# A transformer block on one core: another order of the preparation, and where three batches' MLP rows are normalised and turned

## The chip, the cores and the metric

The kernel runs on one core of a Trainium2 chip. The metric is the device time of one execution in microseconds (us), lower is better. An execution has five engines that run side by side, each through its own list of instructions: TensorE (PE), VectorE (DVE), ScalarE (ACT), GpSimd (POOL) and SyncE (SP), which here only sends transfers (DMAs).

## The reference, cut to what matters

There are 16 batches of 256 tokens with 256 features, 16 heads of 16, an MLP of 1024, and a context of 256 tokens for each batch. All in float32.

```python
c_proj = silu(c) @ W_mod + b_mod
shift_a, scale_a, gate_a, shift_m, scale_m, gate_m = split(c_proj, 6)
modulate = lambda t, shift, sc: t * (1 + sc[:, None]) + shift[:, None]

qkv = modulate(ln(x), shift_a, scale_a) @ W_qkv + b_qkv          # self attention
x = x + gate_a[:, None] * (attention(qkv) @ W_proj + b_proj)

q_c, kv_c = ln(x) @ W_qc + b_qc, ln(context) @ W_kvc + b_kvc      # cross attention
x = x + attention(q_c, kv_c) @ W_cproj + b_cproj

h = gelu(modulate(ln(x), shift_m, scale_m) @ W_mlp1 + b_mlp1)     # MLP
x = x + gate_m[:, None] * (h @ W_mlp2 + b_mlp2)
```

## The kernel before

**Products.** A float32 operand is cut in a high part (a type that TensorE multiplies in one pass) and a low part (the rest). A product is then three: high by high, high by low, low by high. `xTh` and `xTl` are the two parts of a batch's normalised rows, turned so that features lie on the partitions; `Wq`, `Wk`, `Wv` and the others are pairs (high, low). An operand that is turned by TensorE goes through PSUM with a tile named `psT_...`.

**Three stages.** (1) A *preparation* turns the condition, makes the modulation's columns, splits the first weights and makes Q, K and V of the first units. (2) 32 *units* follow, 16 of self attention ("s") and 16 of cross attention ("c"), each with eight beats; beat k of unit n makes scores for unit n+1 (`s`), exponentials' inputs for unit n (`st`), and pieces of the products of units around them. Q and K stand in three big buffers `big[0..2]`, in rows that transfers fill from tiles `h_q`, `l_q`, `h_k`, `l_k` (high and low parts); the fourth kind of row, and all that is not written, is zero, so that each buffer is filled with zeros first. (3) The *MLP* of 16 batches follows in 64 chunks of 256 hidden features: a chunk has the first product (`ph`, twelve matmuls), the GELU (twice on ACT, `hf` and `hh`, and the difference `hl` on POOL) and the second product (twelve matmuls into `s` or `st`). Chunks 0 to 6 of batches 0 and 1 are begun in the last units.

**The order is written out by hand.** Every engine runs its instructions in the order of the program. Strings of words hold that order, and each word issues one step on whatever engines it needs:

- `PRE` is the preparation. `load` sends the first loads from SP; `ld2` loads the third batch; `lg`, `lc`, `lp` load weights that are used later; `z0kp`, `z0qp` and so on fill a half of a big buffer with zeros on POOL (suffix p) or ACT (suffix a; a copy of a zero tile); `bN` runs N warm-up matmuls of zeros on TensorE; `silu` and `turn` make `sT`, the turned silu of the condition (times 1/2); `L0a` and `L0b` are the layer norm's statistics and its `rs` (a power on POOL), `L0d` the normalised rows on DVE; `scale`, `sc1` and `shift` make the modulation's columns `cpT`; `T0t`, `T0h`, `T0l` turn the rows and cut them; `hik`, `lok` split W_k; `K0a`, `K0m` are the two halves of K's product, `K0h`, `K0l` its high and low rows, `K0x`, `K0yp`, `K0w` the three transfers (p: sent by POOL). `bk`, `bq`, `bv` make the biases that the shift adds.
- `SL` places further steps after given beats; `(-1, k)` are the beats before the first unit.
- `BE` is the seam from the attention to the MLP: `Gj`, `Fj`, `Sj` are GELU, first and second product of chunk j; `xb`, `bb`, `sb`, `pb`, `ab` load batch b's rows, add a bias row to them, take the statistics, the power, and the normalised rows; `Tb` turns them by TensorE, `rb` and `gb` are residual and gates; `aT aL C CF` belong to the last attention.

After `BE` a loop runs over the chunks from 12 on. In it a batch's rows are turned in one of two ways, by `TURN`: below it by TensorE (`mlp_T`, four turns, after rows that ACT normalised), from it on without TensorE (`mlp_turn`: DVE transposes blocks of 32 x 32, and four transfers move the blocks; `mlp_scaled` and `mlp_rows` then make both parts).

Loads and stores go through SP's one queue. The tiles of `big`, `wself` and `wcross` are used again by the MLP: `wcross` holds its rows (`ROWS`), `big[2]` the second weights.

Of the kernel before, what the change touches and what calls it, by code (L numbers as in the profile page):

```python
# [16 lines left out]
P = 128  # L17
# [4 lines left out]
def pixart_block(  # L22
# [31 lines left out]

    E_ = {'CUT': 8, 'LN': {'s': 'pool', 'c': 'pool', 'q': 'pool'}, 'ON': (1, 1, 1), 'L0': -16, 'L1': 1, 'S0': -7, 'A0': 0, 'T0': 1, 'S1': 5, 'A1': 7, 'L2': 9, 'T1': 9, 'S2': 32, 'AP': 99, 'DV': (0, 1), 'HP': (1, 0), 'BZ': {}, 'AV': {1: [(1, 2), (1, 3)], 9: [(0, 0), (0, 1)]}, 'AHEAD': (0, 0, 0, 0, 0, 2), 'TW': {(21, 6): 'cb', (23, 5): 'u0', (23, 7): 'u1', (25, 2): 'u2', (27, 3): 'u3', (27, 7): 'h2a', (28, 0): 'l2 h0p u5', (28, 2): 'h1p', (28, 4): 'h3p', (28, 7): 'u4 u6', (29, 0): 'l3d', (29, 1): 'l0', (29, 2): 'l1', (29, 7): 'h5p', (30, 1): 'u7 h6d h7p', (30, 3): 'h4p', (31, 1): 'l4 l6d', (31, 2): 'l5d x2', (31, 4): 'l7', (31, 7): 'b2'}, 'BE': 'G0 av P g0 A1 G1 G2 N1 F7 g1 S0 PF s2 p2 G3 a2 aT aL G4 x3 b3 S1 S2 T2 C r0 G5 S3 G6 S4 s3 CF x4 F8 g2 G7 S5 F9 p3 S6 G8 a3 r1 G9 F10 G10 T3 g3 b4 x5 x6 S7 s4 F11 S8 S9 F12 G11 p4 a4 F13 r2 S10 G12', 'XP': 1, 'IL': 1, 'MF': 0, 'SH': 4, 'RAMP': 1, 'HA': 1, 'MP': 16, 'W': (7, 1, 0, 0), 'PRE': 'load L0a z0kp z0qp L0b silu b15 hik turn L0d brow bp z1qa lok T0t lg scale b1 lc sc1 bro2 T0h T0l shift b3 ld2 one0 hiq loq L1a hiv K0a L1b bk K0m L1d bq K0h K0l Q0a L2a T1t T1h lp K0yp K0x z1kp Q0m T1l bv K1a Q0h K0w Q0x Q0yp Q0l lov K1b Q1a Q0w L2b Q1b K1l V0a K1y Q1l z2ka ld3', 'SL': {(-1, 0): 'V0b wm one1 L2c', (-1, 1): 'V1a T2t T2h', (-1, 2): 'K1wp T2p', (-1, 3): 'K1xp L3a Q1yp V1b ga', (-1, 4): 'M0 z2qa Q1xp Q1wp pb L3b vone gs', (-1, 5): 'mods0 ld4', (-1, 6): 'K2a K2m L3p', (-1, 7): 'L3c cb lx gm', (0, 0): 'sp3 mods1', (0, 1): 'sp0', (0, 3): 'sp1', (0, 4): 'sc2', (0, 6): 'one2', (1, 1): 'sp2', (1, 2): 'sp4'}}

# [41 lines left out]
    BQ, BK, BQC, BKC = 32, 34, 36, 38  # L98
    c_sb, th = [work.tile([B, 2, H], F32, tag=t, name=n, bufs=3)[:, 0] for t, n in (("qkh", "c_sb"), ("qkl", "th"))]
    SP.dma_start(c_sb, cond)  # L100
# [84 lines left out]
    def f_silu():  # L185
        ACT.activation(dummy, mhalf, AF.Tanh)
        ACT.activation(th, c_sb, AF.Tanh, scale=0.5)
        DVE.scalar_tensor_tensor(th, th, 1.0, c_sb, ALU.add, ALU.mult)

    def f_turn():  # L190
        pst = st[:, 1, 480:]
        for k in range(KC):
            PE.transpose(pst[:, k * B:(k + 1) * B], th[:, k * P:(k + 1) * P], ident[:B, :B])
        ACT.mul(sT.rearrange("p k b -> p (k b)"), pst[:, :KC * B], 0.5)

# [102 lines left out]
    wm = []  # L298
# [224 lines left out]
    def to_stack(W, src, bias, dst, which, name):  # L523
# [8 lines left out]
        def first():  # L532
            o.ps = ps_gen(f"ps_{name}", LONG)
            mm3(o.ps[:, 0:N], W, 0, src.xT)

        def third():
# [362 lines left out]

    TURN = 6  # L900

# [85 lines left out]
    def mlp_second(b, c):  # L987
# [15 lines left out]
        if done and b < B - 1:  # L1003
            for t in range(NT):
# [8 lines left out]

    steps = {"x": mlp_load, "b": mlp_bias, "s": mlp_stats, "p": lambda b: M[b].ln.pow(), "a": mlp_apply,
             "r": mlp_residual, "g": mlp_gates, "T": mlp_T, "F": lambda j: mlp_first(j // NCH, j % NCH),
             "G": lambda j: mlp_gelu(j // NCH, j % NCH), "S": lambda j: mlp_second(j // NCH, j % NCH)}
# [46 lines left out]
    for n, v in (("0", u0), ("1", u1), ("2", u2)):  # L1063
        word["T" + n + "t"], word["T" + n + "h"], word["T" + n + "l"] = v.T[0].parts
        word["T" + n + "p"] = v.T[0].low_pool
        for c in "KQ":
            o = getattr(v, c)
            word[c + n + "l"] = o.parts[2]
            word[c + n + "m"], word[c + n + "h"] = o.third, o.high
# [11 lines left out]
    for n in range(3):  # L1081
        for h, c in enumerate("qk"):
            for e, q in (("", DVE), ("p", POOL)):
                word[f"z{n}{c}{e}"] = lambda n=n, h=h, q=q: q.memset(big[n][:, h].bitcast(F32), 0.0)
            word[f"z{n}{c}a"] = lambda n=n, h=h: ACT.copy(
                big[n][:, h].rearrange("p k (a c) -> p (k a) c", c=P),
                wz.unsqueeze(1).to_broadcast([P, 16, P]))
# [12 lines left out]
    word["vone"] = lambda: [POOL.memset(v[:, :, :, HD:], 1.0) for v in vts]  # L1100
    for n, f in (("load", f_load), ("silu", f_silu), ("turn", f_turn), ("brow", f_brow), ("bp", f_bp), ("bro2", f_bro2),
                 ("scale", f_scale), ("sc1", f_sc1), ("shift", f_shift),
# [187 lines left out]
    for i, (b, c) in list(enumerate(chunks))[12:]:  # L1290
# [90 lines left out]
```

## Time and profile before

| what | value |
|---|---|
| runs | 727.61, 727.65, 729.59 us; median 727.65 |
| the profiled execution | 728.29 us; span from its first to its last instruction 726.5 us; mean granted TensorE clock 0.997 |
| PE busy | 718.9 us (99%), 10086 matmuls |
| PE weight loads busy | 633.3 us (87%) |
| DVE busy | 567.8 us (78%) |
| ACT busy | 579.3 us (80%) |
| POOL busy | 526.8 us (73%) |
| DMA | 90.56 MB, mean 125 GB/s |

How to read it: the profile gives the busy time of each engine, and the chain of work that ended last, followed back from the last instruction. Nearly all source lines are those of one helper (line 51), so instructions are told apart by their tiles, written output<-inputs. "PE" is TensorE's matmuls, "PEld" its weight loads, "SPq" and "POOLq" the sequencers that issue transfers. A number in front of a tile's name in a timeline is the start in us from the span's start, then the time that the group took. In square brackets stands the idle time of the engine ahead of the group and what ended it. The granted clock is the share of TensorE's full clock that the chip allowed.

### The profile page before, as it was taken

Reading aid. Unit: us, or ns where it says so; the run is one execution under the profiler, and the core shown is the slowest. Engines: PE = TensorE matmul, PEld = TensorE weight load, DVE = VectorE, ACT = ScalarE, POOL = GpSimd, SP = SyncE. Lnnn points to the kernel's source line nnn. Section 1 sums busy time; section 2 is a strip of 40 time slices with the busy share of each in tenths; the row PEclk is TensorE's granted clock in tenths of the full one; section 3 lists DMA queues with packets and bytes.
Section 4 is the critical chain, followed back from the end, with each engine's and each line's share of the span. In section 5 each row is a group of like instructions: output and inputs, shape, how many; then the busy total and the mean of one; then the engine's idle time right before and its main releaser. Section 6 shows DMA issues by size and latency. Waiting matters only on the chain.

```text
span 726.5 us, 24914 instructions
## 1 busy us (share of the span) xinstructions
PE 718.9 (99%) x10086; PEld 633.3 (87%) x10086; DVE 567.8 (78%) x1208; ACT 579.3 (80%) x1006; POOL 526.8 (73%) x561
## 2 busy tenths in 40 slices
PE   9999999999999999999999999999999999999997
PEld 8788888888888888888888888888878999999997
DVE  4888898989888888888889888888845675676552
ACT  5578898888888888888888888898887677777773
POOL 6766687969687786969687898979746756656643
PEclk9999999999999999999999999999999999999999
DMA  6645333332424343342433444244311414334421
GB/s 208 209 150 176 119 120 143 138 120 105 162 107 161 124 152 124 120 147 112 169 119 137 152 149 161 106 145 142 128 52 54 117 46 117 96 87 111 102 64 39
DMA packets 67110, 90.56 MB, mean 125 GB/s; under 512 B 6194, under 2 KB 38740, under 8 KB 66996
## 3 DMA queue, kind: packets, MB, share of 16 engines
q1 hardware_dynamic: 66164, 86.88, 35.8%
q8 instruction: 80, 1.31, 0.7%
q0 software_dynamic: 560, 1.84, 0.7%
q14 instruction: 34, 0.28, 0.1%
q10 hardware_dynamic: 272, 0.26, 0.1%
HBM read 26.97 MB, written 8.46 MB: 49 GB/s over the span
## 4 chain that ended last, share of the span: by engine, by line
PE 93%; POOL 3%; issue 1%; DVE 1%; ACT 1%; DMA 0%; POOLq 0%; ACTq 0%
PE s L51 18%; PE o L51 16%; PE st L51 15%; PE ph L51 10%; PE ps_P_s L51 4%; PE ps_qc L51 4%; PE ps_v_c L51 4%; PE ps_kc L51 4%; PE ps_q L51 4%; PE ps_v_s L51 3%; PE ps_k L51 3%; PE ps_P_c L51 2%; PE psT_q L51 1%; PE psA_s L51 1%; POOL hl L51 1%
## 5 line engine op out<-in xcount | busy, mean ns | idle before, releaser
L51 DVE TENSOR_REDUCE mx<-s 128x2 f32<-128x512 f32 x504 | 324.7, 683 | 64.3 <-PE s L51 59.0
L51 ACT ACTIVATE pt<-st 128x1024 f32<-128x1024 f32 x252 | 258.9, 1028 | 16.9 <-PE st L51 10.5
L51 PE MATMUL s<-big 63*128 63x256 f32 (+1 forms) x1024 | 185.6, 299 | 0.2
L51 PEld LDWEIGHTS s<-big 63*128 63x128 f32 (+1 forms) x1024 | 133.5, 186 | 19.1 <-DVE l_kc L51 6.6
L51 PE MATMUL st<-big 64*128 64x256 f32 (+1 forms) x1024 | 134.4, 299 | 0.5 <-DMA big<-l_q 0.3
L51 POOL TENSOR_TENSOR hl<-hf,hh 128x512 fp32r<-128x512 f32 x64 | 87.4, 1368 | 63.2 <-ACT hh L51 63.1
L51 PE MATMUL o<-pt,v 128*32 128x256 f32 x2048 | 123.8, 382 | 0.0
L51 PEld LDWEIGHTS st<-big 64*128 64x128 f32 (+1 forms) x1024 | 96.3, 187 | 16.0 <-issue 13.0
L51 PEld LDWEIGHTS o<-pt,v 128*32 128x32 f32 x2048 | 60.0, 109 | 41.4
L51 PE MATMUL ph<-wcross,wself 128*128 128x256 f32 x672 | 85.4, 277 | 0.0
L51 PEld LDWEIGHTS ph<-wcross,wself 128*128 128x128 f32 x672 | 80.4, 188 | 0.0
L51 ACT COPY oT<-o 128x512 f32<-128x512 f32 x63 | 37.0, 587 | 32.7 <-PE o L51 32.7
L51 ACT ACTIVATE hf<-ph,bT 128x256 f32<-128x256 f32 x114 | 47.7, 472 | 18.4 <-PE ph L51 18.4
L51 ACT ACTIVATE hh<-ph,bT 128x256 fp32r<-128x256 f32 x114 | 47.9, 473 | 17.9 <-PE s L51 8.7
L51 PE MATMUL ps_kc<-xTh_c,wcross 64*128 64x256 f32 x256 | 46.6, 291 | 0.0
L51 PE MATMUL s<-big,hh 128*128 128x256 f32 x256 | 45.2, 277 | 0.0
L51 PE MATMUL st<-big,hh 128*128 128x256 f32 x256 | 45.2, 277 | 0.0
L51 PE MATMUL ps_v_c<-wcross,xTh_c 64*128 64x256 f32 x256 | 44.3, 292 | 0.0
L51 PE MATMUL ps_k<-xTh_s,wself 64*128 64x256 f32 (+1 forms) x232 | 43.5, 293 | 0.0
L51 PE MATMUL ps_qc<-xTh_q,wcross 64*128 64x256 f32 x256 | 41.2, 280 | 0.0
L51 PE MATMUL ps_q<-xTh_s,wself 64*128 64x256 f32 (+1 forms) x240 | 40.7, 287 | 0.0
L51 POOL TENSOR_SCALAR xn_c<-c,mv_c,rs_c 128x256 f32<-128x256 f32 x32 | 39.0, 1227 | 1.7
(240 smaller groups left out, 2135.7 us busy)
## 6 DMA issues: line engine op xcount, KB each, us to landing
big<-h_kc SPq DMA_DIRECT2D x32, 256.0 KB
big<-h_qc SPq DMA_DIRECT2D x32, 256.0 KB
big<-h_k SPq DMA_DIRECT2D x30, 256.0 KB
big<-h_q SPq DMA_DIRECT2D x29, 256.0 KB
g<-gd SPq DMA_DIRECT2D x16, 256.0 KB
c<-in_ctx_dram SPq DMA_DIRECT2D x16, 256.0 KB
big<-l_kc SPq DMA_DIRECT2D x16, 256.0 KB
big<-l_qc SPq DMA_DIRECT2D x16, 256.0 KB
```

What stands on the lines that cost most here:

```text
L51: i = f(*a, **k)
```

## The change

*In the preparation* the condition is turned by TensorE before the silu, not after it: `silu` now issues the two turns, and Tanh and the halving on ACT work on the turned 128 x 32 columns; a new step `th2` makes the product on DVE. POOL fills one half buffer and a half of another (`z0kp`, `z1kAp`) ahead of the power, where it filled two; ACT fills a half buffer (`z1qa`) right after the silu, and another (`z0qa`) later. The first K is made by new steps `K0i` (the four high-by-high products, both halves) and `K0j` (the other eight), with the shift columns between them; then follow `bk`, `K0h` and so on. The loads `ld2`, `lg`, `lc`, `lp` are all issued ahead of the transfers of K. The statistics of the third batch (`L2a`) move from before to after the first Q. The warm-up matmuls go from `b15`, `b1`, `b3` to `b5`, `b3`, `b1`, `b1`.

*In the seam* the rows of batches 2 and 4 are normalised by ACT (new words `N`, two small steps on POOL that make -mean x rs, and `e`) instead of by DVE (`a2`, `a4`). Batch 4's bias, statistics and power move ahead; batch 5's bias, statistics, power and `N` are added.

*In the loop* `TURN` is 5 instead of 6: batch 5 is turned by DVE and transfers, no longer by TensorE.

```diff
-'BE': 'G0 av P g0 A1 G1 G2 N1 F7 g1 S0 PF s2 p2 G3 a2 aT aL G4 x3 b3 S1 S2 T2 C r0 G5 S3 G6 S4 s3 CF x4 F8 g2 G7 S5 F9 p3 S6 G8 a3 r1 G9 F10 G10 T3 g3 b4 x5 x6 S7 s4 F11 S8 S9 F12 G11 p4 a4 F13 r2 S10 G12'
+'BE': 'G0 av P g0 A1 G1 G2 N1 F7 g1 S0 PF s2 p2 N2 G3 aT aL e2 G4 x3 b3 S1 S2 T2 C r0 G5 S3 G6 S4 s3 CF x4 F8 g2 G7 S5 F9 p3 S6 G8 a3 r1 G9 F10 b4 G10 T3 g3 x5 x6 s4 p4 N4 S7 F11 S8 S9 F12 G11 e4 b5 F13 r2 S10 s5 G12 p5 N5'
-'PRE': 'load L0a z0kp z0qp L0b silu b15 hik turn L0d brow bp z1qa lok T0t lg scale b1 lc sc1 bro2 T0h T0l shift b3 ld2 one0 hiq loq L1a hiv K0a L1b bk K0m L1d bq K0h K0l Q0a L2a T1t T1h lp K0yp K0x z1kp Q0m T1l bv K1a Q0h K0w Q0x Q0yp Q0l lov K1b Q1a Q0w L2b Q1b K1l V0a K1y Q1l z2ka ld3'
+'PRE': 'load z0kp b5 silu L0a th2 z1kAp L0b z1qa b3 brow bp L0d scale sc1 b1 T0t hik lok T0h bro2 b1 K0i T0l shift K0j z1kBp hiq loq ld2 lg one0 lc lp z0qa L1a L1b bk L1d K0h hiv K0l Q0a bq K0yp K0x T1t T1h K0w Q0m T1l Q0h bv K1a Q0x Q0yp Q0l Q0w lov L2a K1b Q1a L2b Q1b K1l V0a K1y Q1l z2ka ld3'
...
     def f_silu():
         ACT.activation(dummy, mhalf, AF.Tanh)
-        ACT.activation(th, c_sb, AF.Tanh, scale=0.5)
-        DVE.scalar_tensor_tensor(th, th, 1.0, c_sb, ALU.add, ALU.mult)
-
-    def f_turn():
         pst = st[:, 1, 480:]
         for k in range(KC):
-            PE.transpose(pst[:, k * B:(k + 1) * B], th[:, k * P:(k + 1) * P], ident[:B, :B])
-        ACT.mul(sT.rearrange("p k b -> p (k b)"), pst[:, :KC * B], 0.5)
+            PE.transpose(pst[:, k * B:(k + 1) * B], c_sb[:, k * P:(k + 1) * P], ident[:B, :B])
+        ACT.activation(th[:, :KC * B], pst[:, :KC * B], AF.Tanh, scale=0.5)
+        ACT.mul(th[:, KC * B:2 * KC * B], pst[:, :KC * B], 0.5)
+
+    def f_th2():
+        DVE.scalar_tensor_tensor(sT.rearrange("p k b -> p (k b)"), th[:, :KC * B], 1.0, th[:, KC * B:2 * KC * B],
+                                 ALU.add, ALU.mult)
...
+        def some(products):
+            for n, (a, k, f) in enumerate(products):
+                PE.matmul(o.ps[:, f * N:(f + 1) * N], W[a // 2][:, k, f * P:(f + 1) * P], src.xT[a % 2][:, k],
+                          start=(a == n == 0), stop=(a == 2 and k == KC - 1), skip_group_check=True)
+
+        def high_high():
+            o.ps = ps_gen(f"ps_{name}", LONG)
+            some([(0, k, f) for k in range(KC) for f in range(2)])
+
+        def rest():
+            some([(a, k, f) for a in (1, 2) for k in range(KC) for f in range(2)])
+
+        o.by_part = high_high, rest
...
-    TURN = 6
+    TURN = 5
...
+             "N": lambda b: M[b].ln.shift(), "e": lambda b: M[b].ln.steps[2]("act"),
...
+            for i, part in enumerate("AB"):
+                word[f"z{n}{c}{part}p"] = lambda n=n, h=h, i=i: POOL.memset(
+                    big[n][:, h, 4 * i:4 * i + 4].bitcast(F32), 0.0)
...
-            if TURN < b + 4 < B:
+            if 6 < b + 4 < B:
                 mlp_load(b + 4)
```

More of the change, by code (lines that the diff above doesn't have):

```diff
@@ L98, in pixart_block @@
     BQ, BK, BQC, BKC = 32, 34, 36, 38
-    c_sb, th = [work.tile([B, 2, H], F32, tag=t, name=n, bufs=3)[:, 0] for t, n in (("qkh", "c_sb"), ("qkl", "th"))]
+    c_sb, th = [work.tile([p, 2, H], F32, tag=t, name=n, bufs=3)[:, 0]
+                for p, t, n in ((B, "qkh", "c_sb"), (P, "qkl", "th"))]
     SP.dma_start(c_sb, cond)
@@ L1068, in pixart_block @@
             word[c + n + "l"] = o.parts[2]
+            word[c + n + "i"], word[c + n + "j"] = o.by_part
             word[c + n + "m"], word[c + n + "h"] = o.third, o.high
@@ L1100, in pixart_block @@
     word["vone"] = lambda: [POOL.memset(v[:, :, :, HD:], 1.0) for v in vts]
-    for n, f in (("load", f_load), ("silu", f_silu), ("turn", f_turn), ("brow", f_brow), ("bp", f_bp), ("bro2", f_bro2),
+    for n, f in (("load", f_load), ("silu", f_silu), ("th2", f_th2), ("brow", f_brow), ("bp", f_bp), ("bro2", f_bro2),
                  ("scale", f_scale), ("sc1", f_sc1), ("shift", f_shift),
```

2 lines of the change are left out of this document (1 added, 1 removed).

## The prediction

> **What bounds the kernel now.** I read the page first, for the busy shares and the chain that ended last.
>
> ```profile
> PE 718.9 (99%) x10086; PEld 633.3 (87%) x10086; DVE 567.8 (78%) x1208; ACT 579.3 (80%) x1006; POOL 526.8 (73%) x561
> PE 93%; POOL 3%; issue 1%; DVE 1%; ACT 1%; DMA 0%; POOLq 0%; ACTq 0%
> ```
>
> TensorE is the bound: it is busy 99% of the span and holds 93% of the chain. A change pays only where TensorE waits, works at a reduced clock, or has work taken away. To find those places I read the busy time by stretches.
>
> ```profile
> 4.89:8.30 3.41, 3.23 (x28) 2.82 (x27) 0.95 (x3) 2.01 (x5) 2.66 (x4) 1.00 1.01 328
> 39.03:42.44 3.41, 3.41 (x39) 3.41 (x38) 1.98 (x3) 2.22 (x4) 2.48 (x4) 0.50 0.63 243
> 582.00:717.00 135.00, 135.00 (x1193) 135.00 (x1192) 82.83 (x172) 101.77 (x242) 78.41 (x73) 1.00 0.33 85
> ```
>
> Columns: stretch, its length, busy us (and instructions) of PE, PEld, DVE, ACT, POOL, then granted clock. The last 135 us have TensorE full to the hundredth, so whatever it is spared there, or before it, shows at the end. The middle row is a stretch of 3.41 us in which the granted clock was 0.50. The first row looks busy but is not product work: much of it is waiting turns and warm-up matmuls. So the two places to look at are the preparation and the seam before the last 135 us. Here is the preparation, by the timeline (start, length, engine, operation, count, then the idle time before it and its releaser).
>
> ```profile
> 1.04 5.44 PE L51 MATMUL s<-wz 128*128 128x128 f32 x30 [1.04 <-DVE wz L51]
> 1.79 3.55 POOL L51 MEMSET big<- 128x2048 f32 x2
> 3.18 0.41 ACT L51 ACTIVATE th<-c_sb 16x256 f32<-16x256 f32 x1 [0.47 <-DMA c_sb<-in_cond_dram]
> 3.81 0.75 DVE L51 BATCH_NORM_STATS2 st_s<-x 128x6 f32<-128x256 f32 x2 [2.56 <-DMA x<-in_x_dram]
> 4.48 0.30 DVE L51 BATCH_NORM_AGGREGATE mv_s<-st_s 128x2 f32<-128x6 f32 x2
> 5.42 0.23 POOL L51 TENSOR_SCALAR rs_s<-mv_s 128x2 f32<-128x2 f32 x1
> 5.73 0.71 POOL L51 TENSOR_TENSOR rs_s<-rs_s,mhalf 128x2 f32<-128x2 f32 x1
> 6.29 0.66 ACT L51 CAST wself<-wf 128x512 fp32r<-128x512 f32 x1 [2.70 <-DMA wf<-in_L_xcond_W_qkv_dram]
> 6.48 0.74 DVE L51 TENSOR_SCALAR xn_s<-x,mv_s,rs_s 128x256 f32<-128x256 f32 x2 [1.38 <-POOL rs_s L51]
> 6.86 0.18 ACT L51 ACTIVATE sT<-st 128x32 f32<-128x32 f32 x1
> 7.34 1.89 ACT L51 CAST big<-wz 128x2048 fp32r<-128x2048 f32 x1
> 9.58 0.84 ACT L51 ACTIVATE xTh_s<-psT_s,sc 128x256 fp32r<-128x256 f32 x2
> 10.45 0.88 DVE L51 SCALAR_TENSOR_TENSOR xTl_s<-psT_s,sc,xTh_s 128x256 fp32r<-128x256 f32 x2 [1.08 <-ACT xTh_s L51]
> 12.76 0.19 DVE L51 TENSOR_TENSOR bqkv<-st,bT 128x32 f32<-128x32 f32 x1 [0.47 <-PE st L51]
> 13.57 0.84 ACT L51 ACTIVATE h_k<-ps_k,bqkv 128x256 fp32r<-128x256 f32 x2 [2.07 <-PE ps_k L51]
> 17.41 0.87 DVE L51 SCALAR_TENSOR_TENSOR l_q<-ps_q,bqkv,h_q 128x256 fp32r<-128x256 f32 x2
> 20.25 2.44 POOL L51 TENSOR_SCALAR xn_s<-x,mv_s,rs_s 128x256 f32<-128x256 f32 x2
> ```
>
> From the chain in order of time, the lengths of TensorE's groups, and the transfer at its end:
>
> ```profile
> 6.96 0.87 PE psT_s L51 x4
> 11.88 0.84 PE st L51 x8
> 14.37 0.81 PE ps_q L51 x6
> 15.18 0.45 PE psT_s L51 x4
> 18.30 2.69 DMA big<-l_q
> 21.13 0.50 PE st L51 x4
> 23.87 0.45 PE psT_s L51 x4
> ```
>
> The first score tile, at 21.13, opens the main part. It waits for the transfer of l_q (sent at 18.30), which waits for DVE's l_q at 17.41, and so back through h_k at 13.57 to xTh_s at 9.58. That one was late because ACT filled a quarter of `big` with zeros from 7.34 to 9.23, after idling 2.70 us for a load.
>
> **Preparation, step by step.** *Turning the condition.* Before: Tanh (3.18), DVE, two turns, ACT. After: two turns as c_sb lands at 3.18, then Tanh and a product on ACT on 32 columns, 0.18 each by the sT row, then DVE on 32 columns (0.19 by the bqkv row). With 0.4 for the turns (an estimate: the four of the 15.18 row take 0.45), ACT is done near 4.0, while DVE is in the statistics until 4.56. DVE then does the product (4.75) and the two aggregations of 0.30: 5.05. The product is ahead of the aggregations now, which costs 0.2.
>
> *POOL.* Two zero fills held it until 5.34; rs_s started at 5.42. One and a half of them end at 1.79+2.67=4.46, so rs_s starts at 5.1 when its input is there, and ends 1.02 later (5.42 to 6.44): 6.1. xn_s follows at 6.15 to 6.9 instead of 6.48 to 7.22.
>
> *ACT.* The zero fill (1.89) goes into ACT's idle time, 4.0 to 5.9; two copies (under 0.6) and the 0.66 split of the weights end near 7.15. On DVE cpT and sc1 follow xn_s at 0.19 each: 7.3. The turns of xn_s end near 7.5. So xTh_s starts at 7.5 instead of 9.58 and ends at 8.35.
>
> *First products.* K0 now begins with the four that need neither xTl_s nor the low weights: 8.4 to 8.95 (0.135 each, from the ps_q row); the shift columns 0.84 to 9.8; the other eight 1.08 to 10.9; bk 0.84 to 11.7; the addition 0.19. h_k starts at 12.0, not 13.57: 1.6 earlier. Then Q0 (0.81), bq (0.84), the turns (0.45) and Q0's rest (0.81) end at 14.6; xTh_s and h_q of 0.84 each end at 15.5; xTl_s and bv's addition leave l_q at 15.75 against 17.41. It is sent at 16.65 and lands 2.69 later, at 19.35. TensorE's own work up to there (bv, then K1, Q1 and half of V0, 30 products) ends near 19.5. The first score tile moves from 21.13 to about 19.45: **1.7 us earlier**. The nine calls of warm-up matmuls that go (19 become 10, two rows each) are counted at nothing: they stood in time in which TensorE waited.
>
> *What is moved past what.* SP sends the same loads as before, all ahead of the first h_k, which comes at 12.8 at the earliest; the order among them changes only behind the weights, so none of the operands above is later. The second q fill moves to ACT (1.89, about 9.0 to 10.9) and ends a microsecond before h_k. POOL loses the fill between its two sends. The statistics of the third batch move behind the split of Wv on DVE: rs_s then ends near 19.2 and its normalised rows (2.44) near 21.7, when TensorE, 1.7 early, wants them at 22.2 (23.87 before): 0.5 of cover is left, and beyond it TensorE waits. Bounds of this part: 0 if every gain is met by such a wait, 2.1 if all of xTh_s's lead reaches the tile; I take the 1.7 that the chain of rows gives.
>
> **The seam, step by step.**
>
> ```profile
> 555.95 2.67 DVE L51 TENSOR_SCALAR xn_m<-x,mv_m,rs_m 128x256 f32<-128x256 f32 x2 [1.48 <-POOL rs_m L51]
> 558.04 0.27 PE L51 MATMUL psT_m<-ident,xn_m 128*128 128x128 f32 x1
> 558.68 0.55 PE L51 MATMUL psT_m<-ident,xn_m 128*128 128x128 f32 x3 [0.37 <-DVE xn_m L51]
> 559.27 1.21 PE L51 MATMUL psP_c<-wcross,xTh_ac 128*128 128x256 f32 x8
> 580.69 0.27 PE L51 MATMUL psT_m<-ident,xn_m 128*128 128x128 f32 x1
> 581.60 1.62 PE L51 MATMUL ph<-wcross,wself 128*128 128x256 f32 x12
> 592.59 0.60 PE L51 MATMUL psT_m<-ident,xn_m 128*128 128x128 f32 x4
> 592.94 1.63 PE L51 MATMUL ph<-wcross,wself 128*128 128x256 f32 x12
> L51 ACT ACTIVATE xn_m<-x,nb_m,rs_m x22: 594/597/612, 590.7 to 692.3; 128x256 f32<-128x256 f32 x22
> L51 POOL TENSOR_SCALAR nb_q<-mv_q x3: 248/249/253, 90.8 to 493.4; 128x2 f32<-128x2 f32 x3
> L51 POOL TENSOR_TENSOR nb_q<-nb_q,rs_q x3: 194/195/195, 91.1 to 493.7; 128x2 f32<-128x2 f32 x3
> ```
>
> Three turns of MLP rows show the price. Batch 5 (592.59 to 592.94) takes TensorE 0.35 when nothing is late. Batch 2 takes 1.23 (558.04 to 559.27), since DVE's two normalisations last 2.67 and the second turn waits; batch 4 takes 0.91 (580.69 to 581.60). So lateness costs 0.88 and 0.56.
>
> After: batch 2's rows on ACT. rs_m ends at 555.95; POOL's two small steps add 0.25+0.19: 556.4; ACT takes two of 0.60: 557.6, before 558.04. DVE, free of the 2.67, has the low half of the attention rows ready, which the products at 559.27 need. Gain **0.88**. ACT's next GELU is 1.2 later and POOL's hl behind it too, but its product stands behind 12 turned products and more (3 us on TensorE). Batch 4: its bias, statistics and power all move ahead of the GELU of chunk 11, and the 1.2 us lie in an idle stretch of ACT, so its rows are there before TensorE: **0.56**. If the new ACT work came a GELU late, TensorE would lose what it wins here, so 0 is that term's lower end. Batch 5: four turns leave TensorE: 0.35, and the semaphore start of the product behind them, taken as 0.1 (its first row is the long one): **0.44**. Instead DVE transposes and four transfers run as for batches 6 to 15, eight chunks ahead of use: hidden; without that cover their few microseconds would stand in TensorE's path.
>
> **Sum.** 1.7+0.88+0.56+0.44=3.6 from the profiled execution's 728.29: 724.7. That execution is 0.64 above the median 727.65; measured like the median it is **724.1**.
>
> **A rule against it.** The row at 39.03 shows the clock at 0.50 for 3.41 us, after a stretch in which the first exponentials left TensorE little to do. A stretch of that kind costs up to half its length, 1.7. The Trainium skill, "TensorE: Matmul & The Clock Gate", Part 1, says that a free-running window of about 3.4 us of activity sets the clock, and that an idle window halves it; Part 4 adds that turns by TensorE do not count as activity. By that rule the stretch from 4.8 to 8.4, which after the change holds ten small matmuls, four turns and a few warm-ups, would put K0 and Q0 at half clock, and the sum would be 1.7 less. The length of the 39.03 row agrees; that turns do not count no run here shows.
>
> **The rivals.**
> (a) *One more stretch at half clock in the preparation.* For it: 20 rows of warm-up matmuls instead of 38, and a thin stretch from 4.8 to 8.4. Against: the kernel before was thin at 6.5 to 10 too and kept its clock, as the window row 4.89:8.30 has it. Price up to 1.7: 725.8.
> (b) *The preparation's lead is not passed on*: the third batch's rows, or the running maximum on DVE, hold TensorE again before the main part. For it: the 0.5 of cover. Against: TensorE, not DVE, is what the chain goes through from 21.13 on. Then only the seam counts: 727.65-1.88=725.8.
> (c) *Slower: the clock is not granted for the whole preparation.* If the ten rows of warm-up before 3.2 do not suffice, and no stretch until the main part does, some 60 products from 8.4 to 19.5 take double their 0.11 to 0.135, 6 to 8 us more: 728 to 732 in all, 730 in the middle. It decides from the third such stretch on (2 x 1.7 is still covered by 3.6). Against: the warm-up and its rest, 0.18 each by the 1.04 row, fill most of 1.0 to 4.8.
> (d) *The thin stretch at 36 to 39, shifted, escapes the half clock*: 1.7 more gained, 722.4.
>
> **How the numbers follow.** Forecast 0.55, (a) 0.17, (b) 0.15, (c) 0.05, (d) 0.08. No change is told from a change at 0.3%, 2.2 us: faster means under 725.5. The forecast and (d) are faster; (a) and (b) stand at the bound and are halved, less a little for a price below its upper end: faster 0.78, same 0.17, slower 0.05. The range leaves out (c) and the far ends: 722.3 to 726.6; the forecast's own is 723.2 to 725.1.
>
> **What would show it.** xTh_s of the first batch near 7.5, h_k near 12, the first score tile near 19.5; turns of batches 2 and 4 that take 0.35 with no wait for xn_m; no turn of batch 5 by TensorE, and chunk 20's products without a wait for its rows. A granted clock of 0.50 between 8 and 20 means (a) or (c). If xTh_s is early and TensorE idles between 20 and 37, (b) holds. I am wrong if a wait that I put at nothing (GELU after batch 2's or 4's rows, the third batch's rows) appears before TensorE.

## The result, and the profile after

The changed kernel takes 735.31 us (median of six runs, 732.34 to 738.03), the kernel before beside it 727.65 (727.44 to 729.59): a ratio of 1.0091, 95% interval 1.0065 to 1.0117. The forecast was 724.1, its range 722.3 to 726.6. The six runs stand in two groups, 732.3 to 733.0 and 737.7 to 738.0. The profiled execution is of the second: 737.81, span 735.92, so 9.4 us longer in the span than the one profiled before (726.50).

The page's busy times:

```profile
PE 729.6 (99%) x10064; PEld 644.1 (88%) x10064; DVE 568.4 (77%) x1205; ACT 582.6 (79%) x1011; POOL 526.4 (72%) x567
```

The busy time by stretches, with the columns explained above (stretch, length, the five engines with their instructions, granted clock):

```profile
8.30:20.00 11.70, 11.70 (x56) 11.18 (x55) 4.96 (x15) 4.83 (x9) 3.94 (x6) 1.00 0.44 141
24.57:27.99 3.42, 3.42 (x18) 3.42 (x17) 1.54 (x6) 0.84 (x2) 2.46 (x4) 1.00 0.34 129
612.00:717.00 105.00, 105.00 (x894) 105.00 (x893) 67.31 (x133) 78.39 (x188) 59.02 (x54) 1.00 0.34 90
```

The kernel before, in the same view, in the first of these stretches:

```profile
8.30:20.00 11.70, 11.70 (x98) 11.41 (x99) 7.81 (x27) 6.25 (x14) 6.31 (x9) 1.00 0.62 216
```

TensorE is busy all through both, but with 56 matmuls instead of 98. The column of the granted clock says 1.00, but it says so ahead of the first clock event, the first moment at which the trace notes a granted clock, and here that event comes at 27.99 us. Until then the clock must be read from the lengths of the matmuls. In the chain in order of time of the changed kernel:

```profile
11.10 1.52 PE st L51 x8
16.03 1.47 PE ps_q L51 x6
25.50 2.56 PE ps_q L51 x12
28.79 0.43 PE st L51 x4
```

The six products of Q0 took 0.81 before and 1.47 now, twelve of Q1 take 2.56 (0.213 each). **TensorE ran the whole preparation at half clock**: rival (c) is what happened. More places stand in the timeline:

```profile
5.91 0.73 DVE L51 TENSOR_SCALAR xn_s<-x,mv_s,rs_s 128x256 f32<-128x256 f32 x2 [1.15 <-POOL rs_s L51]
9.35 0.84 ACT L51 ACTIVATE xTh_s<-psT_s,sc 128x256 fp32r<-128x256 f32 x2 [2.39 <-PE s L51]
16.36 0.84 ACT L51 ACTIVATE h_k<-ps_k,bqkv 128x256 fp32r<-128x256 f32 x2 [3.50 <-DVE bqkv L51]
22.89 0.87 DVE L51 SCALAR_TENSOR_TENSOR l_q<-ps_q,bqkv,h_q 128x256 fp32r<-128x256 f32 x2
562.96 1.09 ACT L51 ACTIVATE xn_m<-x,nb_m,rs_m 128x256 f32<-128x256 f32 x2 [0.40 <-POOL nb_m L51]
564.53 0.60 PE L51 MATMUL psT_m<-ident,xn_m 128*128 128x128 f32 x4
586.29 0.60 PE L51 MATMUL psT_m<-ident,xn_m 128*128 128x128 f32 x4
603.10 1.52 PE L51 MATMUL ph<-wcross,wself 128*128 128x256 f32 x12
609.09 1.09 ACT L51 ACTIVATE wcross<-yT,cpT,sc 128x256 fp32r<-128x256 f32 x2 [2.28 <-DMA yT<-z]
611.69 1.56 PE L51 MATMUL ph<-wcross,wself 128*128 128x256 f32 x11 [0.26 <-ACT hh L51]
```

xn_s starts at 5.91, a little ahead of the forecast's 6.15; from there all that TensorE touches is late: l_q starts at 22.89 (17.41 before), the first score tile at 28.72 (21.13). How far the changed kernel is behind, at the same instructions of both traces:

| place | before | after | behind |
|---|---|---|---|
| first score tile | 21.13 | 28.72 | 7.59 |
| first product with V (`o`) | 43.91 | 50.61 | 6.70 |
| turn of batch 2 | 558.04 | 564.53 | 6.50 |
| turn of batch 3 (batch 2's gain is in) | 570.71 | 576.31 | 5.59 |
| chunk 16 (batch 4's gain is in) | 587.14 | 592.19 | 5.05 |
| chunk 20 (batch 5's gain is in) | 598.49 | 603.10 | 4.62 |
| last matmul | 722.13 | 731.81 | 9.68 |

So: 7.59 lost in the preparation; 0.89 won back, as the half-clock stretch at 39.03 isn't there (seam_only, below, has the preparation of the kernel before without that stretch, and wins 0.99 between the same two places); 0.91, 0.54 and 0.43 won by the three turns; and then **5.06 lost in the last 120 us**, where TensorE got no more work. There the products simply follow each other more slowly. 894 matmuls fit into the 105 us of the last stretch row, 0.1174 each; before it was 1193 in 135 us, 0.1132. In this trace the pace changes at 611.69, where a chunk's first product waited for a GELU, which ACT did late since it stood behind `wcross<-yT`, here the rows of batch 6. Taking 5.06 from 737.81 gives 732.75, so the two groups of runs are most likely those with and without this slow pace; only one run was profiled.

The slow pace isn't new. The kernel before has it too, between the turns of batches 2 and 3: a chunk's twelve products take 1.58 there and 1.52 once TensorE has turned batch 3.

```profile
563.64 1.58 PE L51 MATMUL ph<-wcross,wself 128*128 128x256 f32 x12
570.71 0.60 PE L51 MATMUL psT_m<-ident,xn_m 128*128 128x128 f32 x4
572.53 1.52 PE L51 MATMUL ph<-wcross,wself 128*128 128x256 f32 x12
```

All twenty traces of this case show the same between these two turns, 0.118 us a matmul ahead of batch 3's turn and 0.113 behind it. What is new is that it comes after the last turn and stays to the end.

### The profile page after: what moved, and what is told of

Its sections match the earlier page's. It is cut to its first block, busy times and chain, and to the rows that moved or that the text cites. A ratio compares the mean times of both kernels' runs of the same rounds, so it can differ in the third digit from the quotient of the medians.

```text
span 735.9 us, 24884 instructions
## 1 busy us (share of the span) xinstructions
PE 729.6 (99%) x10064; PEld 644.1 (88%) x10064; DVE 568.4 (77%) x1205; ACT 582.6 (79%) x1011; POOL 526.4 (72%) x567
## 4 chain that ended last, share of the span: by engine, by line
PE 93%; DVE 2%; ACT 1%; DMA 1%; issue 1%; POOL 1%; SPq 0%; ACTq 0%; POOLq 0%
PE s L51 17%; PE o L51 16%; PE st L51 16%; PE ph L51 9%; PE ps_q L51 4%; PE ps_qc L51 4%; PE ps_P_s L51 4%; PE ps_kc L51 3%; PE ps_v_c L51 3%; PE ps_k L51 3%; PE ps_P_c L51 2%; PE ps_v_s L51 2%; PE ps_h L51 2%; PE psT_q L51 1%; PE psA_c L51 1%; PE psA_s L51 1%
## 5 line engine op out<-in xcount | busy, mean ns | idle before, releaser
L51 PEld LDWEIGHTS s<-big 63*128 63x128 f32 (+1 forms) x1024 | 132.7, 185 | 18.9 <-DVE l_kc L51 6.6
L51 PE MATMUL ph<-wcross,wself 128*128 128x256 f32 x672 | 87.7, 280 | 0.3 <-ACT hh L51 0.3
L51 PEld LDWEIGHTS ph<-wcross,wself 128*128 128x128 f32 x672 | 82.6, 189 | 0.5 <-ACT hh L51 0.5
L51 PE MATMUL ps_k<-xTh_s,wself 64*128 64x256 f32 (+1 forms) x232 | 45.0, 303 | 0.0
L51 PE MATMUL ps_q<-xTh_s,wself 64*128 64x256 f32 (+1 forms) x240 | 42.4, 292 | 0.0
```

The costliest lines, as they stand in the source:

```text
L51: i = f(*a, **k)
```

## The experiments

All times are medians with the lowest and the highest run; the kernel before, run beside them, had medians of 728.0 to 728.4 us. "Seam" stands for the changed `BE` and `TURN`, "preparation" for the changed `PRE` with its new steps.

**1. The two parts apart: seam_only and prep_only.**

```diff
 seam_only:  'BE' and TURN of the changed kernel, the rest of the kernel before
 prep_only:  'PRE' and its steps of the changed kernel, 'BE' and TURN of the kernel before
```

> The kernel before with the change's seam and loop (BE, TURN 5), and the old preparation. If the seam does what its three terms say and the preparation alone is to blame: 725.8 (1.9 less than before). If the loop's loss in the profile after (TensorE's products 118 ns apart instead of 113 from 611 us to the end, 5 us in all, begun by one wait for a GELU) comes with batch 5's way of turning: 725.8 in some executions and about 731 in others, and the profile of a long one has the 118 ns from a wait on. If the loop's loss comes from the preparation or from the run: 725.8 in all.

> The change's preparation with the old seam and TURN 6. Clock theory (no stretch of 3.4 us is full of products before the second batch's K and Q, so TensorE works at half clock until about 28 us): first score tile near 28.7 us against 21.1, 734.3 in all. Rival, the order of the preparation is slower by itself (ACT's or DVE's waits): also later, but then with products 0.113 us apart; the spacing of ps_k's and ps_q's products tells, 0.21 or 0.11.

seam_only: 726.69 (725.54 to 730.86), ratio 0.9985 (0.9962 to 1.0008). prep_only: 734.89 (726.10 to 739.60), ratio 1.0061 (1.0031 to 1.0090). The loss of the first 7 us comes with the preparation. The seam's turns, in the timeline of seam_only:

```profile
557.41 0.60 PE L51 MATMUL psT_m<-ident,xn_m 128*128 128x128 f32 x4
569.18 0.60 PE L51 MATMUL psT_m<-ident,xn_m 128*128 128x128 f32 x4
```

From the first to the second it gains 0.91 on the kernel before (12.67 there, 11.77 here), then 0.54 and 0.46: the three terms of the seam. But two of its twelve runs, with a mean clock of 1.000, lie at 730.5 and 730.9, 5 above the others. They were not profiled; the size is that of the slow pace. The kernel before, with the same preparation, shows no such run: of its some 140 runs beside the experiments none with a mean clock of 0.999 or more lies above 729, but for one stray of 1352.64. So the late slow pace goes with the new seam, though not with it alone: prep_only has the old seam and one run at 739.60, 4 above its neighbours and with a mean clock of 1.000, which was not profiled either.

prep_only has two kinds of runs: four at 726.1 to 729.4 and the others at 733 and above. Its profile is of the first kind (729.16), with the clock granted at 4.89:

```profile
7.83 0.78 PE ps_k L51 x4
11.26 0.80 PE ps_q L51 x6
15.26 0.78 DVE l_q L51 x2
16.10 4.31 DMA big<-l_q
20.55 0.50 PE st L51 x4
```

```profile
18.55:21.96 3.41, 1.42 (x13) 1.17 (x12) 1.75 (x3) 2.30 (x3) 3.12 (x4) 1.00 0.90 295
21.96:25.37 3.41, 3.41 (x16) 2.85 (x18) 1.64 (x3) 0.84 (x2) 0.00 (x0) 0.50 0.58 191
```

With the clock, the chain up to l_q is even earlier than forecast (sent at 16.10, 16.65 in the forecast). Then the transfer takes 4.31, not 2.69, TensorE has little to do meanwhile (1.42 of 3.41 us), and a half-clock stretch follows the thin one: rival (a).

**2. The length of the warm-up, in both directions: before_b5, warm_mid, warm_first.**

```diff
 before_b5:  (kernel before)  - L0b silu b15 hik turn      + L0b silu b5 hik turn
 warm_mid:   (changed kernel) - L0b z1qa b3 brow           + L0b z1qa b10 brow
 warm_first: (changed kernel) - b5 silu L0a th2 z1kAp L0b z1qa b3 brow bp L0d scale sc1 b1 T0t hik lok T0h
                              + b15 z1qa hik silu L0a z1kAp L0b L0d th2 brow bp T0t lok scale sc1 T0h
```

warm_first thus also drops `b3` and one `b1` and moves five steps forward; it isn't the changed kernel with more calls alone.

> The kernel before with 5 calls of warm-up matmuls at the start instead of 15, nothing else. Clock theory: TensorE stays at half clock until the second batch's products as in the change, first score tile 5 to 8 us later, 732 to 735 in all. Rival (the order, not the warm-up): no change or up to 0.3 less than 727.65, as the turns of the condition start earlier.

> The change with 10 calls of warm-up matmuls between the condition's turns and its first columns instead of 3. Clock theory: products are continuous from 3.8 to about 7, so the clock is full by 5 to 9 us; first score tile near 20, and 724 to 725.5 in all (plus 5 in executions with the slow pace in the loop). Rival (the order is slow): stays near 732 or above, since more is put in TensorE's way.

> The changed kernel with its fifteen warm-up calls put back ahead of the new preparation (the new chain, new memory clears and new seam stay). Theory 'warm-up': the clock is granted near 5 us as before the change, the first score tile starts at 19.5 to 20.6 us instead of 28.7, the first o product near 43 instead of 50.6, and the time is 724.5 to 726 in most executions, 10 under the changed kernel; where the loop takes the slower pace, up to 5 more. Rival 'thin preparation': the new order itself is too thin for the clock, warm-up or not: the clock is lost again before 25 us or not granted, and the time stays at 730 or above.

before_b5: 732.89 (732.23 to 734.70), ratio 1.0068 (1.0043 to 1.0094). The old preparation with ten calls fewer, and nothing else, loses 4 to 5 us; its chain:

```profile
13.94 1.28 PE ps_k L51 x6
18.03 0.81 PE ps_q L51 x6
25.30 0.50 PE st L51 x4
```

The half clock lasts until 15.85 (six products of K0 in 1.28, then six of Q0 in 0.81), and the first score tile is at 25.30, 4.17 late; I had expected 5 to 8, with the half clock up to the second batch. So the calls that the forecast counted at nothing buy the clock. But they are not enough for the new order: warm_mid 734.20 (732.69 to 738.87), warm_first 732.75 (731.82 to 738.19), both as slow as the change. warm_first by stretches:

```profile
3.60:7.01 3.41, 3.41 (x18) 3.41 (x18) 1.61 (x6) 1.40 (x3) 1.82 (x3) 1.00 0.84 255
7.01:10.42 3.41, 3.09 (x23) 2.43 (x22) 0.84 (x4) 1.02 (x7) 2.18 (x2) 1.00 1.05 342
10.42:13.84 3.42, 3.10 (x14) 3.10 (x15) 1.20 (x4) 3.26 (x5) 1.30 (x1) 0.50 0.39 124
24.07:27.49 3.42, 3.42 (x18) 3.42 (x18) 2.25 (x8) 0.84 (x2) 1.10 (x3) 0.50 0.60 230
```

Here the clock is granted at 7.01, lost after one thin stretch at 10.42, and granted again only at 27.49, after a stretch of eighteen back-to-back products. My theory "warm-up" alone fell; the rival "thin preparation" was right. warm_mid has the same at 11.83.

**3. What releases the clock and what holds it.** For this I took a share: a matmul of 128 float32 columns or of 256 columns of cut operands counted at 0.21 us at half clock (their spacing there) and at half of that at the full one, shorter ones in proportion, over each 3.41-us stretch. It is an estimate worked out from the traces of all these kernels, good to a few per cent, and for the preparation only. The groups of eight matmuls on 16 columns look busy (1.52 us at half clock in the chain above) and count for 0.2. The clock was released after stretches of 75% (before_b5), 78, 79, 82 to 88 and 100%; it was not after 77% (after_reset), 74% (the changed kernel) and less. The border lies near three quarters, as closely as the estimate tells; the two sides overlap between 75 and 77%. Once granted, it was kept through 40 to 45% and taken away after 27% (warm_mid), 30 (first_t6), 34 (seam_t6) and 36% (warm_first, prep_only). One trace doesn't fit: after_rows lost it at 21.88 after a stretch of 41 to 45%, in which the main part begins already (at 20.05); this border isn't sharp either. The changed kernel's own stretches from 0.69 on have 70, 44, 74, 56, 45, 68 and 59%, then 100%: enough to keep a clock, never enough to get one until the second batch's K and Q. Three kernels raised the share without moving the chain's order (after_b9 has the rows of section 5 moved as well):

```diff
 filled_x:   (warm_first)     - bro2 b1 K0i ... Q1l z2ka   + bro2 b5 K0i ... Q1l b6 z2ka   and the early load of 4
 fill_mid_x: (warm_mid)       - bro2 b1 K0i ... Q1l z2ka   + bro2 b8 K0i ... Q1l b6 z2ka   and the early load of 4
 after_b9:   (changed kernel) - load z0kp b5 silu          + load z0kp b9 silu
                              - bro2 b1 K0i                + bro2 b5 K0i                   and the rows of 5
```

> The changed kernel with fifteen warm-up calls first, five more where TensorE waits ahead of the first K product and six more behind the second batch's last projection, where it waits for the l_q transfer; and the early load of x. Theory 'thin preparation': the stretch that took the clock away at 10.4 us is filled to some 50%, the clock granted near 5 to 7 us stays, the first score tile starts near 21 instead of 28.7, and most executions lie at 725 to 727. Rival: the clock is not what costs the 7 us; they stay at 731 and above.

> The changed kernel with ten warm-up calls instead of three behind the cond turn, eight more ahead of the first K product, six more behind the second batch's last projection, and the early load of x. With ten in the middle alone the clock was granted at 5.0 us and lost at 11.8 us behind a stretch streamed to 27%, in which TensorE waited 1.6 us. Theory 'thin preparation': that wait is filled, the clock stays in most executions, and these lie at 725 to 727.5; a few whose first 3.4 us stretches fall badly stay at 731 to 733. Rival: the clock is lost all the same or was not the cause: all at 731 and above.

> The changed kernel with nine instead of five warm-up calls first, five instead of one ahead of the first K product, and the same move of ACT's rows. Theory 'length against phase': the dense start is 5.7 us long instead of 4.1, a 3.41-us stretch fits whole into it in (5.7 - 3.41) / 3.41 = two thirds of the executions instead of one fifth to one quarter; so about eight of twelve get the clock before 10 us and lie at 725 to 727.5, the other third at 731.5 to 733.5. Rival: the share doesn't change (one in four), or all get it or none, and the phase is not what decides.

filled_x: 727.84 (727.18 to 735.03); fill_mid_x: 727.79 to 730.63, median 728.57. Ten and thirteen dummy calls more than in warm_first and warm_mid, and 5 to 6 us are gone: the clock was the loss. (The early load, which they also have, changed nothing by itself: after_x in 4.) But the long warm-up delays the chain (first score tile at 22.57 and 24.50), so nothing is won over the kernel before. after_b9 (731.76, 727.23 to 735.36) has the clock at 5.64 and the tile at 21.08; its time is spoiled by the rows moved as in section 5. I expected eight of twelve runs with the early clock; a late clock would put a run at 737 or above there (732.3 and the 4.8 of section 5), and none of the twelve lies so high, so all twelve seem to have got it early. The border near 75% would explain it: a stretch needn't fit whole into the dense start.

**4. What starts the late slow pace: seam_t6, first_t6, after_reset, after_x, seam_x.**

```diff
 seam_t6:     (seam_only)      TURN = 6, BE without 'b5 s5 p5 N5': batch 5 turned by TensorE
 first_t6:    (warm_first)     the same
 after_reset: (changed kernel)
              if b + 1 < TURN:
                  mlp_T(b + 1)
+             else:
+                 PE.transpose(ps_gen(f"pace_{b}", SHORT)[:, :P], ident, ident)
 after_x, seam_x: (changed kernel, seam_only) mlp_load(b + 4) moved from c == 1 to c == 0, ahead of the turn
```

> Old preparation, the new seam for batches 2 and 4 alone, batch 5 turned by TensorE as before the change. Theory 'turn sets the pace': the last turn of TensorE, near 591 us, starts the loop at 113 ns a product, so no execution carries the 3 to 5 us that four of twelve showed with batch 5 turned by VectorE; the two seam gains of 0.9 and 0.54 stay, the 0.45 of batch 5 goes: 726.0 to 726.7, with a narrow spread. Rival 'pace by chance': the slower pace comes as often as without this turn, and a third of the executions lie at 730 or above.

> Fifteen warm-up calls ahead of the new preparation, the new seam for batches 2 and 4, batch 5 turned by TensorE as before the change. Theory 'warm-up and turn': the preparation gains 0.6 to 1.7 us and the seam 1.4 over the kernel before: 724.8 to 726.2, without a second group of executions. Rival 'thin preparation': the clock is lost between 20 and 25 us and the gain of the preparation with it: 726.2 to 727.5.

> The changed kernel with one more turn of a 128 by 128 constant by TensorE at the start of each batch of the loop (13 of them, 0.12 to 0.25 us each, 1.5 to 3 us). Theory 'turn sets the pace': the products go at 113 ns from each turn on, a slow stretch lasts one batch at most (0.43 us), the group of executions at 737.7 goes, and all lie at 733.5 to 736. Rival 'pace by chance' (or by the late transfer alone): two groups remain, 5 us apart, the upper one at 739 to 741.

> The changed kernel with the load of x for four batches on issued at the start of each batch of the loop, ahead of the four turn transfers and of the output's transfer, instead of behind them. Theory 'late load': the wait that starts the slow pace (rows of batch 6 late, because DVE's turn stands behind a bias that waits for x) goes, so does the group of executions at 737.7, and nearly all lie at 732 to 733. Rival 'late for another reason' (the turn transfers themselves, or chance): half the executions still lie 5 us above the others.

> The kernel before with the new seam alone (batch 5 turned by VectorE) and the load of x issued at the start of each batch of the loop. Theory 'late load': no execution with the full clock lies at 730 or above, all that keep the clock lie at 725.3 to 726.2, the others up to 1.5 us above for each half-clock stretch. Rival 'chance': two to four of twelve at 730 or above at the full clock.

seam_t6: 727.38 (726.72 to 733.43). Its profile (733.43) has the slow pace although TensorE turned batch 5 just before:

```profile
595.18 1.02 ACT L51 ACTIVATE wcross<-psT_m,cpT,sc 128x256 fp32r<-128x256 f32 x2 [1.37 <-DVE xTf_m L51]
598.68 1.56 PE L51 MATMUL ph<-wcross,wself 128*128 128x256 f32 x11 [0.25 <-ACT hh L51]
```

Again a first product waits for a GELU that ACT did late, here behind batch 5's rows. "A last turn sets the pace for good" fell. first_t6, at 735.08 (727.05 to 739.55), has the same wait, 0.25 at 603.59, and the slow pace from there; its clock is granted at 6.04, lost at 12.87 and granted again at 26.52. In after_reset, 734.90 (728.82 to 738.78), with a turn in each batch:

```profile
612.00:717.00 105.00, 105.00 (x927) 105.00 (x926) 67.29 (x133) 79.87 (x191) 59.97 (x55) 1.00 0.36 91
```

927 matmuls where the changed kernel had 894: the fast pace in this execution, as expected, at 0.12 us a turn. But three runs at 737.3 to 738.8 don't fit. That a turn ends the slow pace stands in other traces: at batch 3's turn in all twenty, and in before_b5, which falls into it behind the turn of batch 4 at 584.87, at batch 5's turn at 597.18.

The early load changed nothing: after_x 732.55 (726.58 to 738.87), three of twelve at 737.7 and above; seam_x 726.52 (725.88 to 731.12), one of twelve 5 us above. "Late load" is not the cause. In after_x's profile the load is early and the rows late all the same:

```profile
594.66 2.49 SPq L51 DMA_DIRECT2D yT<-z  x4
600.45 1.09 ACT L51 ACTIVATE wcross<-yT,cpT,sc 128x256 fp32r<-128x256 f32 x2 [2.34 <-DMA yT<-z]
603.04 1.68 PE L51 MATMUL ph<-wcross,wself 128*128 128x256 f32 x12 [0.32 <-ACT hh L51]
```

seam_x, without the slow pace, at the same place:

```profile
596.43 2.84 SPq L51 DMA_DIRECT2D yT<-z  x4
600.91 1.09 ACT L51 ACTIVATE wcross<-yT,cpT,sc 128x256 fp32r<-128x256 f32 x2 [1.05 <-DMA yT<-z]
601.58 1.52 PE L51 MATMUL ph<-wcross,wself 128*128 128x256 f32 x12
```

The turn transfers were issued alike and landed 1.3 us later in after_x. In after_x and in the changed kernel a 16 KB packet of an instruction queue ran behind the four issues, 3 us after the first, and took 1.47 and 1.39 us; in seam_x and seam_only it came 0.9 and 1.9 after the first and took 0.96. That is what the traces show; it was not tried by itself.

Nor is the late GELU needed. after_fill (6) takes the slow pace at 626.19 after a gap of 0.06 us, with no such packet near, and warm_mid at 593.16 with no gap at all: the products there go on at 0.118 where those just ahead went at 0.113. What starts it stays open.

after_x's profile is also the one that has the changed preparation with the clock, granted at 5.23 and not taken away until the end:

```profile
7.98 0.77 PE ps_k L51 x4
11.43 0.80 PE ps_q L51 x6
15.45 0.80 DVE l_q L51 x2
16.26 3.33 DMA big<-l_q
19.72 0.50 PE st L51 x4
```

**5. The rows out of the way: seam_rows, after_rows.**

```diff
-            if ahead[0]:                        # at c == 3
-                mlp_rows(ahead[0])
+        if c == 0 and TURN <= b + 1 < B:        # one chunk later
+            mlp_rows(b + 1)
```

> The kernel before with the new seam (batch 5 turned by VectorE), and in the loop ACT's rows of a batch moved from the end of the batch two ahead to behind the first gelu of the batch one ahead, so that the gelu doesn't stand behind a late turn transfer. Theory 'late rows': TensorE's wait for a gelu at the start of batch 4 or 5 goes, and with it the executions that lie 5 us above the others at the full clock (3 of 24 with this seam so far): 725.3 to 726.2 at the full clock, 1 to 5 more only where the mean clock is below 0.998. Rival 'chance': one to three of twelve still at 730 or above with a mean clock of 0.999 or more.

> The changed kernel with the same move of ACT's rows in the loop. Theory 'late rows': the executions at 737 to 739 go (6 of 18 so far in the changed kernel and with its early load); what is left are those with the clock near 28 us, at 732 to 733.5, and about one in four with the clock near 5 us, at 724.3 to 727. Rival 'chance': a third of the executions stay at 737 to 739.

seam_rows: 732.22 (730.82 to 742.63); after_rows: 739.97 (734.14 to 740.93). It misfired: batch 5's low half, on DVE, now comes behind other DVE work, TensorE waits 2.04 for it at 599.22 in seam_rows, and a half-clock stretch follows; together 4.8 us at one place (chunks 19 and 20 take 10.23 there, 5.44 in seam_only). No verdict on the slow pace.

**6. The version that follows: after_fill, prep_fill, after_fill_x.** The changed kernel with nine warm-up calls first and five ahead of K0: as it is, with the old seam, and with the early load.

```diff
-'PRE': 'load z0kp b5 silu L0a th2 ... T0h bro2 b1 K0i
+'PRE': 'load z0kp b9 silu L0a th2 ... T0h bro2 b5 K0i
```

> The changed kernel with nine instead of five warm-up calls first and five instead of one ahead of the first K product; nothing else. With these the trace of the kernel that also moved ACT's rows had the clock at 5.6 us, the first score tile at 21.08 and the turn of batch 2 at 556.84 (558.04 before the change). Theory 'clock': ten or more of twelve executions have the clock before 10 us; without a slow loop they lie at 727.65 - 1.2 - 1.9 = 724.5 to 725.5, with it 5 above; the median lies at 724.5 to 726. Rival: the clock is missed as often as in the changed kernel, and the median stays above 730.

> The same preparation with the old seam (batch 5 turned by TensorE). Theory 'clock': 727.65 - 0.6 to - 1.2 = 726.4 to 727.1 in most executions, none 5 us above at the full clock, since the old seam showed none in over 60. Rival: the median above 730, as the new preparation without the calls (734.9).

> As the first, with the load of x issued at the start of each batch of the loop. Theory 'late load': 724.5 to 725.5 with at most one of twelve at 729 or above. Rival 'late transfers': as many of twelve 4 to 5 us above the others as without the early load.

**after_fill: 725.50 (725.08 to 730.12), ratio 0.9970 (0.9949 to 0.9991): 0.3% faster than the kernel before beside it (728.43), and below all six runs of the changed kernel.** prep_fill: 727.62 (727.15 to 731.01), ratio 0.9991 (0.9976 to 1.0006): no gain clear of noise, and 0.5 above what I expected. after_fill_x: 725.92 (725.45 to 730.51), 0.9966 (0.9936 to 0.9997). None of the 36 runs lies above 731.01, while the fastest of the changed kernel lay at 732.34; without the two numbers changed, 11 of 42 runs with this preparation (the changed kernel, prep_only, after_reset, after_x) were below 730. So eight dummy calls move the median from 734.89 to 727.62 with the old seam, and from 735.31 to 725.50 with the new one; part of the second step is that three of six runs lay in the slower group there and three of twelve do here. With the early load, too, three of twelve still lie 4 to 5 us above the others, where at most one was expected; in after_fill's profile, 729.63, it is the slow pace. The chain of after_fill:

```profile
10.64 0.47 PE ps_k L51 x4
17.78 0.80 DVE l_q L51 x2
18.59 2.65 DMA big<-l_q
21.38 0.50 PE st L51 x4
```

The first score tile is where it was before the change (21.13); in the other traces with these calls it is at 20.38 (prep_fill), 21.08 and 21.11. The calls cost the chain most of what the new order had won.

## Why the prediction was wrong, step by step

**The step that failed: "The nine calls of warm-up matmuls that go (19 become 10, two rows each) are counted at nothing: they stood in time in which TensorE waited."** They did stand in waiting time, and what hid them there was right; but they were what got the clock. before_b5 shows it: ten of these calls out of the old kernel cost 4.17 us at the first score tile. The forecast asked what covers them and not what they hold up. Rival (c) named this with 0.05, and its argument against it ("the warm-up and its rest, 0.18 each by the 1.04 row, fill most of 1.0 to 4.8") was the misreading: most of a stretch isn't enough unless it falls together with a 3.41-us stretch, and that depends on the execution. With the same preparation the stretch from 1.48 in prep_only was filled to 82% and got the clock, and the one from 0.69 in the changed kernel to 70% and didn't. Nor do the calls alone suffice in the new, thinner order: warm_first got the clock at 7.01 and lost it at 10.42. The sign named for (c), a granted clock of 0.50 between 8 and 20, could not show it, as that column says 1.00 ahead of the first event; the lengths did.

**(c)'s price was too small.** It doubled 60 products, 6 to 8 us; on the forecast's 724.1 that makes 730 to 732, not the 728 to 732 written there. With the clock the tile stands at 19.72 (after_x), without it at 28.72: 9.0, since the turns and the columns of the modulation double too. The other 5 us of the profiled run are the slow pace, which no rival had.

**The rule against the change was nearer than its price.** The forecast weighed it as one stretch, 1.7, since the old preparation was thin and kept its clock. The Trainium skill, "TensorE: Matmul & The Clock Gate", Part 1, has the window free-running and 3413 ns long. All traces here agree: clock events lie whole multiples of 3.41 us apart, and the first, where it is early, stands anywhere from 3.87 to 7.81. The 1.7 for one stretch was the step too short: a clock that isn't got at the start is not got in the next stretch either, if the work is thin. Rival (d) came true beside it: the stretch at 39.03 escaped the half clock, but that was worth 0.89 to 0.99, not 1.7.

**The preparation's chain was right where it had its clock.** Forecast, then after_x: first products 8.4, 7.98; l_q 15.75, 15.45; sent 16.65, 16.26; first score tile 19.45, 19.72. The only term off is the transfer: 2.69 forecast, 3.33 in after_x, 4.31 in prep_only. Its last landing trails the others (in prep_only 15 of 16 lie near 18.9, one at 20.41; in after_x one trails by 0.7, in the kernel before none). A 16 KB instruction packet runs ahead of these transfers and took 1.7 us in prep_only, 1.1 in after_x and 0.96 before the change. The order fits; that the packet holds up one of the 16 parts was not tried.

**The seam was right.** 0.88, 0.56, 0.44 forecast; 0.91, 0.54, 0.43 in the changed kernel. In seam_only the turn transfers of batch 5 are hidden as forecast: chunk 20 starts without a wait.

**"TensorE full to the hundredth" was no bound on the last 135 us.** A full TensorE has two paces, 0.113 and 0.117 to 0.118 us a matmul. The kernel before has the slow one only between the turns of batches 2 and 3; the row over its last 135 us is the fast one. The forecast looked for waits, and a pace is none: 0.0047 us more on each of some thousand matmuls is 5 us. The sentence "if the new ACT work came a GELU late, TensorE would lose what it wins here" priced a wait at its own length; in the changed kernel a wait of 0.26 stood where 5 were lost. That the wait is the cause isn't shown: warm_mid took the slow pace without one, and after_fill_x waits 0.17 at 603.95 and is back at the fast pace within the chunk. Nor is batch 5's way of turning: the late rows in the changed kernel were those of batch 6, which are made the same way in the kernel before, and seam_t6, where TensorE turns batch 5, has the slow pace as well. The step is open here.

**What the change is worth.** With the clock and the fast pace it would be near the forecast: after_x's profile, 729.50 with 5.1 of slow pace, leaves 724.4. It is a sum that no run showed: the three after_x runs that seem to have had the early clock without the slow pace took 726.6 to 727.2, and after_fill's 725.1 to 725.8 is the nearest measured.

## What to carry to other kernels

Before warm-up work is shortened, ask what it holds up and not only what hides it: take out the calls alone, as in before_b5, and look at the lengths of the matmuls behind them. Here getting the clock asked for a stretch filled to some three quarters, keeping it for far less, so a thin preparation needs a dense start clearly longer than one stretch, to cover whatever its phase can cost: with five calls first it seems to have got the clock in 11 of 42 runs, with nine and five in all of 36. And a full engine is not always at its best pace: count matmuls in a fixed stretch, in several places.

## What was unexpected of the hardware

- The clock is asymmetric in these preparations: got only after a stretch filled to some three quarters or more, kept through 40 to 45% in most traces, lost after 27 to 36% (estimates from the matmuls' spacing, with one exception at 41 to 45%).
- TensorE's back-to-back matmuls have two lasting paces at the full clock, 929 (seam_x) and 894 (changed kernel) in 105 us. A turn by TensorE ended the slow one wherever one came, in all twenty traces. After the last turn it began in seven traces: in four behind a wait for a GELU of 0.25 to 0.32 us, in after_fill behind a gap of 0.06, in warm_mid and after_b9 behind none. In six it stayed to the end; in after_b9 it ended with the wait of 3.18 and the half-clock stretch that the rows moved as in section 5 bring.
- A step of DVE can be drawn out while POOL works. In warm_mid, moved by the calls, `sc` took 2054 ns (8.36 to 10.41) instead of the 180 of prep_only, while POOL made a low part and cleared (8.20 to 10.38), and K0 waited 1.6 for what hangs on it:

```profile
L51 DVE TENSOR_SCALAR sc<-cpT x1: 2054/2054/2054, 8.4 to 8.4; 128x32 f32<-128x32 f32 x1
```
